# Turning the feed-forward tokens in 32x32 blocks on VectorE, with sixteen DMAs a block, in a macaron transformer layer

## The chip, the cores and the metric

The kernel runs on one core of one Trainium2 chip. The metric is the device time of one execution, in microseconds (us). The five engines of a core (TensorE, VectorE, ScalarE, GpSimd and SyncE; in the profile PE, DVE, ACT, POOL and SP) each run their own instructions in order and wait for each other by semaphores. PEld is TensorE's weight load, and a name with a q at its end (SPq) is an engine's sequencer, which issues DMAs.

## What is computed

A macaron layer in float32 over 16 x 256 tokens of 256 features: half a feed-forward part, attention, another half feed-forward part with the same weights.

```python
x = x + 0.5 * ffn(layernorm(x), w1, b1, w2, b2)
x = x + attention(layernorm(x), Wq, Wk, Wv, Wo)      # 16 heads of 16, causal, rotary
x = x + 0.5 * ffn(layernorm(x), w1, b1, w2, b2)

def ffn(x, w1, b1, w2, b2):        # w1: 1024 x 256, w2: 256 x 1024, both rounded to -1, 0, 1
    h = gelu(x @ ternary(w1).T + b1)
    return h @ ternary(w2).T + b2
```

## The kernel before, in words

The 4096 tokens stay in SBUF through the whole kernel, as 8 blocks (`NBLK`) of 512 tokens (`xs`, line 79): 128 tokens on the partitions, 4 tiles (`BT`) side by side, 256 features in the free dimension. Both feed-forward parts come from one function, `ffn(ln, after)` (line 273), called with ln = 0 and ln = 2. The attention lies between them and is not touched by the change.

A feed-forward part is a sequence of steps `step(u)` (line 373) with u = 8 i + f: block i, and f one of 8 chunks of 128 hidden features. In each step

- `up(i, f)` (line 315) multiplies chunk f of w1 with the block: four matmuls of 128x512 into a PSUM tile m (two such tiles take turns). ScalarE makes the GELU of m twice, as `h_high` (the type float32r, in which TensorE is fast and which keeps fewer bits) and as `h_whole` (float32). VectorE, or GpSimd for f = 1, 3 and 5, subtracts them, which gives `h_rest`, the bits that `h_high` lost.
- `down(i, f - 2)` (line 329) multiplies what was made two steps ago (`LATE` = 2) with w2: eight matmuls of 128x256, tokens as the stationary operand, four token tiles times high and rest. After f = 7 VectorE adds the sum to `xs`, and in the second part two DMAs on SP store the tokens.

The four matmuls of `up` need the tokens of the block the other way round, features on the partitions. The block after the current one is made ready in three places of the steps:

- at f = 3, `prepare(i + 1)` (line 282): four VectorE instructions normalize the four token tiles into `xn`;
- at f = 5 and f = 6, `turn_in(i + 1, k)` (line 291) for the two halves k of the features: TensorE turns four 128x128 squares of `xn` into a PSUM tile `tp`, ScalarE copies `tp` as `high` (`xnT_0`, float32r), VectorE subtracts, which gives `rest` (`xnT_1`);
- `up(i + 1, 0)`, at f = 0 of the next block, is their first reader.

For block 0 of both parts and block 1 of the second part this is called from other places (`begin`, lines 359 to 371, and lines 752 to 771). The steps f = 3, 5 and 6 of blocks 1 to 6 make blocks 2 to 7, in both parts.

All calls go through a wrapper that keeps them in the written order on their engine (`InOrder`, line 159). So an instruction that waits holds back all that stands behind it on its engine. It is also why nearly all instructions have line 167 in the profile, and why they are told apart by their tiles. DMAs are issued by SP, and the framework gives them eight completion semaphores in turn, so that a DMA waits for the one that was issued eight before it.

`flat1` and `flat2` (line 81) are two 128x2048 tiles that first hold the weights w1 and w2 in float32. Later the attention uses `flat1` and the first half of `flat2` for its rotary step (lines 423 to 427); the second half of `flat2` is free once w2 has been rounded, in step 3 of the first part.

Of the kernel before, what the change touches and what calls it, by code (L numbers as in the profile page):

```python
# [8 lines left out]
FP = mybir.dt.float32  # L9
FR = mybir.dt.float32r  # L10
AF = mybir.ActivationFunctionType
# [4 lines left out]
P = 128  # L16
D = 256
KC = D // P
FF = 1024
# [10 lines left out]
def kernel(  # L30
# [17 lines left out]
    BT = 4  # L48
    TB = BT * P
    NBLK = NT // TB  # L50
# [24 lines left out]
    b1_sb = const.tile([P, NFC], FP, name="b1_sb")  # L75
# [5 lines left out]
    flat1, flat2 = (state.tile([P, 2 * FF], FP, name=f"w_{n}") for n in range(2))  # L81
# [19 lines left out]
    for k in range(KC):  # L101
        rows = slice(k * P, (k + 1) * P)
        nc.sync.dma_start(out=wv[:, k, :], in_=wqkvT[rows, 2 * D :])
        for at in range(0, 2 * D, 4 * HD):
            n, j, e = at // D, at // P % 2, at // (4 * HD) % 2
            nc.sync.dma_start(
                out=wqk[:, k, n, j, :, e, :],
                in_=wqkvT[rows, at : at + 4 * HD].rearrange("p (r d) -> p r d", d=HD),
# [20 lines left out]
        out=mask_k,  # L129
        in_=mask_k,  # L130
# [28 lines left out]
    class InOrder:  # L159
# [11 lines left out]
    tensor, vector, scalar, gpsimd, sync = (  # L171
        InOrder(engine) for engine in (nc.tensor, nc.vector, nc.scalar, nc.gpsimd, nc.sync)
    )
# [4 lines left out]
    def stats(ln, n):  # L178
        st = small.tile([P, 6], FP, name="st")
        vector.bn_stats(st, tokens(n))  # L180
        vector.bn_aggr(mv[ln][:, n, :], st)

    def finish_stats(ln, first, n):

        var = small.tile([P, BT], FP, name="var")
        gpsimd.tensor_scalar(
            var[:, 0:n], mv[ln][:, first : first + n, 1], LN_EPS, 1.0, ALU.add, ALU.mult
        )
        gpsimd.tensor_tensor(
            rstd[ln][:, first : first + n], var[:, 0:n], power[:, 0:n], ALU.pow  # L190
        )

    def normalize(ln, n, to, engine=None):
        (engine or vector).tensor_scalar(
            to,
            tokens(n),
            mv[ln][:, n, 0:1],
            rstd[ln][:, n : n + 1],
            ALU.subtract,
            ALU.mult,  # L200
        )
# [30 lines left out]
    def signs(n, of):  # L232

        w, to = of((w1, w2)[n]), of((w1q, w2q)[n])
        vector.tensor_scalar(to, w, half[n][:, 1:2], None, ALU.is_lt)
        vector.scalar_tensor_tensor(
            to, w, half[n][:, 0:1], to.bitcast(FP), ALU.is_gt, ALU.subtract
        )
# [31 lines left out]

    LATE = 2

    def ffn(ln, after):
        xn, xnT, hT, ys = {}, {}, {}, {}

        def measure(i):
            if ln == 0:
                for t in range(BT):
                    stats(0, i * BT + t)
                finish_stats(0, i * BT, BT)  # L280

        def prepare(i, engine=None):
            xn[i] = fp.tile([P, BT, D], FP, name="xn", bufs=1)
            for t in range(BT):
                normalize(ln, i * BT + t, xn[i][:, t, :], engine)
            xnT[i] = [fp.tile([P, KC, TB], FR, name=f"xnT_{n}") for n in range(2)]

        def add_bias(i):
            gpsimd.tensor_add(xs[i], xs[i], b2_sb.unsqueeze(1).to_broadcast([P, BT, D]))

        def turn_in(i, k):
            tp = ps_mm.tile([P, TB], FP, name="mm")
            for t in range(BT):
                tensor.transpose(
                    tp[:, t * P : (t + 1) * P], xn[i][:, t, k * P : (k + 1) * P], ident
                )
            high, rest = (xnT[i][n][:, k, :] for n in range(2))
            scalar.copy(high, tp)
            return lambda: vector.tensor_sub(rest, tp, high.bitcast(FP))

        first = {}

        def up_first(i, f, to=None):
            h = first[i, f] = ps_m.tile([P, TB], FP, name="m") if to is None else to
            for n in range(2):
                for k in range(KC):
                    tensor.matmul(
                        h,
                        w1q[:, k, f * P : (f + 1) * P],
                        xnT[i][n][:, k, :],  # L310
                        start=(n == 0 and k == 0),
                        stop=(n == 1 and k == KC - 1),
                    )

        def up(i, f):
            if (i, f) not in first:
                up_first(i, f)
            h = first.pop((i, f))
            high = fp.tile([P, TB], FR, name="h_high", bufs=LATE + 3)
            rest = fp.tile([P, TB], FR, name="h_rest", bufs=LATE + 3)  # L320
            whole = fp.tile([P, TB], FP, name="h_whole", bufs=3)
            scalar.activation(high, h, AF.Gelu, bias=b1_sb[:, f : f + 1])
            scalar.activation(whole, h, AF.Gelu, bias=b1_sb[:, f : f + 1])

            engine = gpsimd if f in (1, 3, 5) and not (ln == 0 and i == NBLK - 1) else vector
            engine.tensor_sub(rest, whole, high.bitcast(FP))
            hT[i, f] = (high, rest)

        def down(i, f):
            if f == 0 and ln == 2 and i == NBLK - 1:  # L330

                ys[i] = [ps_mm.tile([P, 2, D], FP, name="mm") for t in range(0, BT, 2)]
            elif f == 0:
                y = ps_w.tile([P, BT, D], FP, name="w")
                ys[i] = [y[:, t : t + 2, :] for t in range(0, BT, 2)]
            parts = hT.pop((i, f))
            order = [(t, n) for t in range(BT) for n in range(2)]
            if ln == 2 and (i, f) == (NBLK - 1, NFC - 1):

                order = [(t, n) for n in range(2) for t in range(BT)]  # L340
            for t, n in order:

                tensor.matmul(
                    ys[i][t // 2][:, t % 2, :],
                    parts[n][:, t * P : (t + 1) * P],
                    w2q[:, f, :],
                    start=(f == 0 and n == 0 and t % 2 == 0),
                    stop=(f == NFC - 1 and n == 1 and t % 2 == 1),
                )
            if f == NFC - 1:  # L350
                for t in range(0, BT, 2):
                    xt = xs[i][:, t : t + 2, :]
                    vector.scalar_tensor_tensor(
                        xt, ys[i][t // 2], 0.5, xt, ALU.mult, ALU.add
                    )
                for t in range(0, BT, 2):
                    after(i, t)

        def begin():
            measure(0)  # L360
            if ln == 0:
                sizes(0)
            prepare(0)
            if ln == 0:
                threshold(0)
                signs(0, lambda w: w[:, :, 0 : FF // 2])
            for k in range(KC):
                turn_in(0, k)()
            if ln == 0:
                signs(0, lambda w: w[:, :, FF // 2 :])  # L370
                sizes(1)

        def step(u):
            i, f = divmod(u, NFC)
            if i < NBLK:
                up(i, f)
                if ln == 0 and u == 0:
                    threshold(1)
                if ln == 0 and u in (0, 3):
                    part = slice(0, NFC // 2) if u == 0 else slice(NFC // 2, NFC)  # L380
                    signs(1, lambda w: w[:, part, :])
                if ln == 0 and u == 4:
                    gpsimd.tensor_scalar(b2_sb, b2_sb, 0.5, 0.0, ALU.mult, ALU.add)
                if u == 1:
                    measure(1)
                if ln == 0 and f >= 4 and i + 2 < NBLK:
                    stats(0, (i + 2) * BT + f - 4)
                    if f == NFC - 1:
                        finish_stats(0, (i + 2) * BT, BT)
                if i + 1 < NBLK and (ln, i) != (2, 0):  # L390
                    if f == 3:
                        prepare(i + 1)
                    if f in (5, 6):
                        turn_in(i + 1, f - 5)()
                if f == (1 if i == NBLK - 1 else 6):
                    add_bias(i)
            if u >= LATE:
                down(*divmod(u - LATE, NFC))
            if ln == 0 and u == 2 * NFC + 2:
                make_tables()  # L400
            if ln == 0 and u < (NBLK - 1) * NFC and later:
                later.pop(0)()

        return begin, step, prepare, turn_in, up_first

    FFN_STEPS = NBLK * NFC + LATE
# [12 lines left out]
    xn_a, xnT, qT, kT, o, oT, y_a = {}, {}, {}, {}, {}, {}, {}  # L419
# [326 lines left out]
    rest = []  # L746
    for p in range(8):
# [7 lines left out]
        rest = made  # L755
        if p == 0:
            prepare(0, gpsimd)
    a, z = NB - 2, NB - 1
# [88 lines left out]
```

## Time and profile before

| | us |
|---|---|
| median of three runs | 623.36 (623.34 to 624.16) |
| span of the profiled execution, from the first to the last instruction | 621.8 |
| PE busy | 600.7 (97%) |
| DVE busy | 462.1 (74%) |
| ACT busy | 415.3 (67%) |
| POOL busy | 306.4 (49%) |
| first part, from the first GELU of block 0 to the last GELU of block 7 | 14.5 to 157 |
| second part | 487.3 to 615.7 |
| from the first GELU of a block to that of the next, blocks 3 and 4 of the first part and 2 to 6 of the second | 15.8, 15.8 and 16.1 |

The page lists for each engine how long it was busy. Below it stands the chain of work that ended last, followed back from the last instruction through whatever released each step: engines with a large share there set the time, and time taken from the others gains nothing by itself. The timeline view lists the instructions by start time; in brackets behind an instruction is how long its engine had been idle before it and what ended that.

### The profile page before, as it was taken

What the parts mean: (1) busy time and instruction counts of PE and PEld (TensorE: products, weight loads), DVE (VectorE), ACT (ScalarE), POOL (GpSimd) and SP (SyncE); (2) the same over time, 40 slices, a digit from 0 to 9 for tenths busy, and PEclk for the clock granted to TensorE, in tenths of its full rate; (3) what the DMA queues carried; (4) which work ended last, traced back from release to release, by engine and by line L of the source; (5) the groups of instructions that cost most, each with busy time, mean ns of one, the idle gap of its engine ahead of it and who ended that gap; (6) DMA issues with size and microseconds to landing.
All of it is one profiled execution on the core that took longest, in us unless ns stands there. A gap on an engine that the chain in (4) does not pass through costs nothing.

```text
span 621.8 us, 14721 instructions
## 1 busy us (share of the span) xinstructions
PE 600.7 (97%) x5580; PEld 487.5 (78%) x5580; DVE 462.1 (74%) x1650; ACT 415.3 (67%) x716; POOL 306.4 (49%) x277
## 2 busy tenths in 40 slices
PE   4999999999999999999999999999999999999997
PEld 3798999887667777777777777777766788888886
DVE  6877777785788888888888888888885375555553
ACT  4666766674576667776777677767765666676674
POOL 3655555782464455545564456553442163334443
PEclk9999999999999999999999999999999999999999
DMA  9800000000001000110010001100100011011001
GB/s 286 178 21 1 2 1 18 17 1 18 20 35 38 18 22 35 37 36 21 19 37 36 20 20 36 37 19 21 36 4 2 1 35 35 34 35 35 26 21 56
DMA packets 25478, 21.30 MB, mean 34 GB/s; under 512 B 10944, under 2 KB 21056, under 8 KB 25408
## 3 DMA queue, kind: packets, MB, share of 16 engines
q1 hardware_dynamic: 24848, 19.44, 9.9%
q8 instruction: 44, 0.72, 0.5%
q10 hardware_dynamic: 560, 0.92, 0.4%
q14 instruction: 26, 0.21, 0.1%
HBM read 7.51 MB, written 4.19 MB: 19 GB/s over the span
## 4 chain that ended last, share of the span: by engine, by line
PE 87%; DVE 7%; ACT 2%; issue 2%; POOL 1%; DMA 1%; DVEq 0%; ACTq 0%; POOLq 0%
PE mm L167 37%; PE w L167 28%; PE m L167 21%; DVE h_rest L167 2%; DVE st L167 1%; DVE xn L167 1%; ACT h_high L167 1%; ACT h_whole L167 1%; DVE w2q L167 1%; DMA x<-in_x_dram 1%; DVE mv L167 1%; DVE masked L167 0%; DVE x L167 0%; POOL h_rest L167 0%; POOL rstd L167 0%
## 5 line engine op out<-in xcount | busy, mean ns | idle before, releaser
L167 DVE CUSTOM_DVE_ANT_0 masked<-m,mask_q 128x128 f32<-128x128 f32 x480 | 142.7, 353 | 41.0 <-PE m L167 39.7
L167 PE MATMUL m<-xnT,w1q 128*128 128x512 f32 x504 | 142.5, 404 | 0.9 <-DVE w1q L167 0.9
L167 ACT ACTIVATE h_high<-m,b_sb 128x512 fp32r<-128x512 f32 x126 | 86.7, 688 | 79.2 <-PE m L167 79.2
L167 DVE TENSOR_TENSOR h_rest<-h_whole,h_high 128x512 fp32r<-128x512 f32 x83 | 76.1, 918 | 71.0 <-ACT h_whole L167 70.6
L167 ACT ACTIVATE pT<-w 128x768 f32<-128x768 f32 x128 | 104.1, 814 | 31.6 <-DVE w L167 24.6
L167 PE MATMUL w<-qT,kT 32*128 32x256 f32 (+1 forms) x1024 | 121.7, 349 | 0.8 <-ACT pT L167 0.5
L167 POOL TENSOR_TENSOR h_rest<-h_whole,h_high 128x512 fp32r<-128x512 f32 x45 | 60.3, 1340 | 125.7 <-ACT h_whole L167 125.5
L167 PE MATMUL w<-w2q,h_high 128*128 128x256 f32 x480 | 120.9, 286 | 1.1 <-DVE w2q L167 1.1
L167 PE MATMUL w<-w2q,h_rest 128*128 128x256 f32 x480 | 118.0, 280 | 1.3 <-POOL h_rest L167 1.2
L167 PEld LDWEIGHTS w<-qT,kT 32*128 32x128 f32 x1024 | 90.7, 184 | 32.4 <-issue 26.4
L167 PE MATMUL m<-kT,qT 32*128 32x128 f32 x960 | 114.9, 349 | 0.7 <-ACT kT L167 0.7
L167 PEld LDWEIGHTS m<-xnT,w1q 128*128 128x128 f32 x504 | 86.7, 190 | 16.4 <-DVE xnT L167 2.9
L167 PEld LDWEIGHTS w<-w2q,h_rest 128*128 128x128 f32 x480 | 90.6, 189 | 6.4 <-POOL h_rest L167 1.8
L167 PEld LDWEIGHTS w<-w2q,h_high 128*128 128x128 f32 x480 | 90.4, 188 | 5.8 <-DVE w2q L167 1.6
L167 DVE TENSOR_TENSOR w<-w,mask_k 128x512 f32<-128x512 f32 x128 | 88.9, 695 | 7.1 <-PE w L167 7.1
L167 ACT ACTIVATE h_whole<-m,b_sb 128x512 f32<-128x512 f32 x126 | 85.8, 681 | 0.0
L167 PEld LDWEIGHTS m<-kT,qT 32*128 32x128 f32 x960 | 65.9, 185 | 2.9 <-ACT kT L167 1.6
L167 POOL TENSOR_TENSOR w<-w,cosT 128x512 f32<-128x512 f32 x32 | 41.2, 1289 | 51.9 <-ACT w L167 32.0
L167 PE MATMUL mm<-xnT_a,wqk 128*128 128x256 f32 x256 | 62.2, 386 | 0.0
L167 POOL TENSOR_TENSOR w<-w,sinT 128x512 f32<-128x512 f32 x32 | 40.9, 1278 | 25.7 <-DMA w<-w 25.6
L167 PEld LDWEIGHTS mm<-xnT_a,wqk 128*128 128x128 f32 x256 | 46.2, 190 | 7.6 <-issue 0.7
L167 PE MATMUL mm<-pT,vals 128*32 128x256 f32 (+1 forms) x1024 | 48.2, 329 | 0.3 <-ACT oT L167 0.3
(90 smaller groups left out, 888.0 us busy)
## 6 DMA issues: line engine op xcount, KB each, us to landing
w<-w SPq DMA_DIRECT2D x64, 128.0 KB
out_dram<-x SPq DMA_DIRECT2D x15, 256.0 KB
x<-in_x_dram SPq DMA_DIRECT2D x7, 512.0 KB
w<-in_w2T_dram SPq DMA_DIRECT2D x1, 1024.0 KB
qT<-mT SPq DMA_DIRECT2D x64, 4.0 KB
w<-in_w1T_dram SPq DMA_DIRECT2D x1, 512.0 KB
w<-in_w1T_dram ACTq DMA_DIRECT2D x1, 512.0 KB
wqk<-in_wqkvT_dram SPq DMA_DIRECT2D x16, 32.0 KB
```

The costliest lines, as they stand in the source:

```text
L167: return tc.keep_in_program_order(getattr(self.engine, name)(*args, **kwargs))
```

## The change

For blocks 2 to 7 of both parts (`by_blocks`) TensorE no longer turns the tokens. `prepare` ends with one VectorE instruction that transposes every 32x32 square of `xn` by itself, into the second half of `flat2` (`turned`). Sixteen DMAs on SP then move the squares to where they belong, straight into `xnT_1`; each moves 32 partitions x 2 x 512 bytes, 32 KB. `turn_in` has left a ScalarE copy from `xnT_1` to `high`, and a VectorE subtraction in place on `xnT_1`. The squares arrive in an order in which the tokens of a block are permuted, and the two GELUs put them back by writing through a four-dimensional pattern with runs of 32 elements.

```diff
+    turned = flat2[:, FF:].rearrange("p (j n t) -> p j n t", j=8, n=BT)
+
     def ffn(ln, after):
         xn, xnT, hT, ys = {}, {}, {}, {}
+        by_blocks = range(2, NBLK)
...
             xnT[i] = [fp.tile([P, KC, TB], FR, name=f"xnT_{n}") for n in range(2)]
+            if i in by_blocks:
+                vector.transpose(
+                    turned.rearrange("p j n t -> p (j n t)"),
+                    xn[i].rearrange("p n (j t) -> p j n t", t=32),
+                )
+                for a in range(4):
+                    for j in range(4):
+                        sync.dma_start(
+                            out=xnT[i][1][32 * j : 32 * j + 32, :, a * P : a * P + P].bitcast(FP),
+                            in_=turned[32 * a : 32 * a + 32, j::4, :, :].rearrange(
+                                "p k n t -> p k (n t)"
+                            ),
+                        )
...
         def turn_in(i, k):
+            if i in by_blocks:
+                high, rest = (xnT[i][n][:, k, :] for n in range(2))
+                scalar.copy(high, rest.bitcast(FP))
+                return lambda: vector.tensor_sub(rest, rest.bitcast(FP), high.bitcast(FP))
             tp = ps_mm.tile([P, TB], FP, name="mm")
...
-            scalar.activation(high, h, AF.Gelu, bias=b1_sb[:, f : f + 1])
-            scalar.activation(whole, h, AF.Gelu, bias=b1_sb[:, f : f + 1])
+            for to in (high, whole):
+                if i in by_blocks:
+                    to = to.rearrange("p (n a t) -> p a n t", n=BT, a=4)
+                    of = h.rearrange("p (a n t) -> p a n t", n=BT, a=4)
+                else:
+                    of = h
+                scalar.activation(to, of, AF.Gelu, bias=b1_sb[:, f : f + 1])
```

## The prediction

> **What bounds the kernel now.** I read the page first: busy times, the clock, the chain that ended last.
>
> ```profile
> span 621.8 us, 14721 instructions
> ...
> PE 600.7 (97%) x5580; PEld 487.5 (78%) x5580; DVE 462.1 (74%) x1650; ACT 415.3 (67%) x716; POOL 306.4 (49%) x277
> ...
> PEclk9999999999999999999999999999999999999999
> ...
> PE 87%; DVE 7%; ACT 2%; issue 2%; POOL 1%; DMA 1%; DVEq 0%; ACTq 0%; POOLq 0%
> ```
>
> TensorE is never idle for long and is 87% of the chain. Next, block 3 of the second part: the chain there (start, length), then the timeline of the same stretch (start, time of the group, engine).
>
> ```profile
> 545.17 0.93 PE m L167 x4
> 546.10 0.44 PE mm L167 x4
> 546.54 0.95 PE w L167 x8
> ```
>
> ```profile
> 542.45 1.38 DVE L167 TENSOR_SCALAR xn<-x,mv,rstd 128x256 f32<-128x256 f32 x4
> ...
> 545.94 0.60 PE L167 MATMUL mm<-ident,xn 128*128 128x128 f32 x4
> ...
> 547.30 0.59 ACT L167 CAST xnT<-mm 128x512 fp32r<-128x512 f32 x1
> ...
> 551.49 1.37 PE L167 MATMUL m<-xnT,w1q 128*128 128x512 f32 x4
> ...
> 552.90 0.69 ACT L167 ACTIVATE h_high<-m,b_sb 128x512 fp32r<-128x512 f32 x1 [0.87 <-PE m L167]
> ```
>
> The turning squares (mm) are on the chain: 0.44 us for four. A step without them takes 0.93 + 0.93 = 1.87 us. But look at the dates: the tokens are normalized at 543.83, and the next block's `up` has read them and ended by 552.90. The new path must fit into those 9.1 us. `prepare` stands at f = 3, so only some four steps lie between.
>
> **What is removed.** In 12 blocks (2 to 7, twice) two groups of four squares: 24 x 0.44 = 10.5 us, all on the chain. If everything new were hidden, the time would be 623.4 - 10.5 = 612.9.
>
> **What is added, along its path.** Nothing in the trace turns squares on VectorE or moves 32 KB inside SBUF in 512-byte runs; the nearest DMAs are these, from the SP timeline (first two) and the GpSimd timeline.
>
> ```profile
> 24.99 5.14 SPq L106 DMA_DIRECT2D wqk<-in_wqkvT_dram  x8
> ...
> 170.17 1.15 SPq L167 DMA_DIRECT2D w<-w  x2
> ```
>
> ```profile
> 172.87 1.27 POOL L167 TENSOR_TENSOR w<-w,sinT 128x512 f32<-128x512 f32 x1 [1.41 <-DMA w<-w]
> ```
>
> - *Transpose, 128x1024 float32:* the rows with 1024 elements on VectorE are 0.75 us (tensor_scalar, w1q) and 1.28 (scalar_tensor_tensor, w1q). I take 1.1; ends 0.75 and 2.6 (two passes of the slower row).
> - *Issue:* SP issues one DMA after the other. Of the eight wqk DMAs each also waits on one of the eight completion semaphores in turn, as the new ones will; the quiet ones start 0.55 apart. The pairs inside SBUF take 1.15 for two, the 64 qT ones 0.50 in the median, the output stores 0.37. I take 0.53; ends 0.43 and 0.60. The sixteenth starts 15 x 0.53 = 7.95 us after the first.
> - *Landing:* the second DMA of the pair at 170.17 starts at 170.72, and GpSimd, which waits for it, starts at 172.87: 2.15 for 128 KB. For 32 KB I take 2.0, ends 1.6 and 2.2. All sixteen are needed, as each brings a part of both halves k.
> - *Behind the landing:* ScalarE is in order, so its copy at f = 5 holds back the GELUs of f = 6, those the copy of the second half. Copy 0.59 (the CAST row), two GELUs 1.26 (from 550.76 to 552.02), copy 0.59, VectorE's subtraction 0.69, the last matmul of `up(i + 1, 0)` 0.4: 3.53. A copy from SBUF instead of PSUM, eight semaphores to wait on and the GELUs' output pattern are costed at nothing; the nearest row for SBUF input on ScalarE (qT, 128x256 in 0.50, against 0.37 for the same size from PSUM) makes it up to 0.13 for each copy, and I allow 0.1 for each GELU.
>
> From the end of normalizing to the end of `up(i + 1, 0)`: 1.1 + 0.05 (SP woken) + 7.95 + 2.0 + 3.53 = 14.6 us. Before it is the time from the fourth `xn` to the next block's first h_high. In block 3 of the second part: 543.83 + 14.6 = 558.5 against 552.90, 5.6 late. The same working at each f = 3 gives 7.3, 5.7, 7.3, 7.3, 2.2, 8.2 in blocks 1 to 6 of the first part (block 5 has attention matmuls there for cover; in block 6 normalizing takes until 127.43) and 6.8, then five times 5.6, in the second. Sum: 38.1 + 34.6 = 72.7 us. The removed 10.5 is already in it, as the dates of before hold it.
>
> It does not come back later: the next normalizing stands behind h_rest(2) of the next block on VectorE, so the path closes into a ring once a block. In the gap TensorE has `up(6)`, `up(7)` and `down(5)` left, then waits. Queues: on SP the two stores of a block (540.40) are issued before the sixteen, and the rotary pairs of the first part stand between series with 8 us of room. VectorE's own backlog (some 13 us a block) runs beside the ring.
>
> **The clock.** TensorE will now idle 5 to 7 us a block. What that does is seen at both ends of the trace (PE timeline; then stretches, PEclk third from the end).
>
> ```profile
> 11.86 2.04 PE L167 MATMUL m<-xnT,w1q 128*128 128x512 f32 x4 [0.86 <-DVE w1q L167]
> ...
> 21.16 1.09 PE L167 MATMUL m<-xnT,w1q 128*128 128x512 f32 x4
> ```
>
> ```profile
> 617.20:619.80 2.60, 0.00 (x0) 0.00 (x0) 1.17 (x2) 0.00 (x0) 0.00 (x0) 1.00 0.43 145
> 619.90:621.70 1.80, 0.00 (x0) 0.00 (x0) 0.00 (x0) 0.00 (x0) 0.00 (x0) 0.50 0.19 64
> ```
>
> Less than 2.8 us after the last matmul the granted clock is 0.50. At the start matmuls begin 0.43 us apart until 15.7 us and 0.23 after, that is, 3.9 us from the first dense ones, 7.5 from TensorE's first instruction. So after each gap some 4 us pass at half speed and lose 2.0; ends 0 and 3.7 (the two steps between `up(i + 1, 0)` and the next h_rest(2) at half speed, after which the loss is hidden). 12 x 2.0 = 24 us.
>
> Sum against the profiled execution: 621.8 + 72.7 + 24 = 718.5. The median stands 1.6 above the span (what lies around it), which gives **720 us**.
>
> Two rules of the Trainium skill bear on this. In "DMA: Bandwidth & Descriptors", section "Issuing engines are not separate DMA queues", the sequencer's time to start a DMA is called usually small beside the DMA; the rows say otherwise here (0.53 x 16 against one landing of 2). Taken at its word, with issue free, the path would be 8 us shorter, no block late, and the time 613. The same page's rules for kernel authors speak against the change: transfers under 64 KB are mostly overhead. "TensorE: Matmul & The Clock Gate", Part 1, has the clock fall after one idle window of about 3.4 us and rise after one such busy window; by it the loss would be 1.7 to 3.4 a gap, 20 to 41 in all, where the rows gave 24.
>
> **Rivals.**
> - *Hidden after all, faster: 612.9.* It decides by the issue pace: with the mean lateness of 6.1 us a block, it breaks even at 0.53 - 6.1 / 15 = 0.12 us a DMA and no clock loss. No row is under 0.37. 5%.
> - *Late, but the clock holds* (idle cut up by the GELUs and first matmuls, or issue at 0.43 and a shorter landing): 621.8 + 72.7 + 1.6 = 696, with the fast issue down to 680. For it: `up(6)` and `up(7)` still fall into the gap. Against it: what is left of the gap is twice the 2.8 us. 20%.
> - *The ring of semaphores sets the pace:* each DMA waits for the eighth before it, and where landings grow longer SP slows down. The eight wqk DMAs from 16.76 on took 7.64 us, 0.95 apart, beside the big loads. That would add 15 x 0.42 = 6.3 a block, 76 in all: 796. Against it: SBUF is quiet then, and eight issues last 4.2 us, twice a landing. 12%.
> - *The change does not do it:* the instruction order of the changed kernel shows the 24 groups gone from PE, twelve transposes on DVE and 192 DMAs on SP. No more than 1% for a time within 0.2%, about what a measurement of this kernel can tell from no change.
>
> **Numbers.** Forecast 62%, and with the second rival 82%. The range takes in both, the unknown ends above (issue 0.60: +12; transpose 2.6: +18; clock: +20, not all at once) and stops short of the ring: 680 to 765. Faster 5%, same 1%, slower 94%.
>
> **What would show it.** SP's sixteen issues lasting 8 us or more (if 2 us, I am wrong at the root); ScalarE's copy waiting for DMA, 5 us or more; PE idle before `up(i + 1, 0)` twelve times; matmuls 0.43 apart behind each gap, PEclk at 5 or between; blocks of 15.8 and 16.1 us grown to some 24; attention as long as before.

## The result, and the profile after

| | us |
|---|---|
| before, median | 623.35 (623.32 to 624.16) |
| after, median of four runs | 744.73 (742.47 to 745.12) |
| ratio after / before | 1.193 [1.192, 1.195] |
| profiled execution of after | 742.47, span 740.7 |

The kernel is 19% slower; the forecast was 720 us, in a range of 680 to 765. The page of after, in the lines that were shown of before and with the row of TensorE's slices:

```profile
span 740.7 us, 14986 instructions
...
PE 617.8 (83%) x5484; PEld 498.3 (67%) x5484; DVE 462.4 (62%) x1662; ACT 415.0 (56%) x716; POOL 301.9 (41%) x277
...
PE   5949648668599999999999999999999477558657
...
PEclk9989779789699999999999999999999797889789
...
PE 67%; SPq 15%; DVE 6%; ACT 5%; DMA 4%; issue 3%; POOL 1%; ACTq 0%; DVEq 0%; POOLq 0%
```

The same row of TensorE's slices before:

```profile
PE   4999999999999999999999999999999999999997
```

Read the slices (the busy share of each fortieth of the span, in tenths) from left to right: TensorE and its clock have holes at both ends, in the two feed-forward parts, and are untouched in the middle, in the attention. The row of the chain names what came in: SP's sequencer, which had no share before, has 15% of the span, and DMA went from 1% to 4%. TensorE has fewer matmuls (96 squares less) and is still busy for longer, as part of it ran at a lower clock.

One block, the chain of after from the end of the transpose on (start, length, what):

```profile
627.35 0.95 PE w L167 x8
628.29 0.58 SPq L167
628.87 0.05 issue
628.92 0.59 SPq L167
...
637.23 0.59 SPq L167
637.82 0.04 issue
637.87 1.89 DMA xnT<-w
639.75 0.02 issue
639.78 0.62 ACT xnT L167
640.39 0.59 ACT h_high L167
640.98 0.59 ACT h_whole L167
641.57 0.04 issue
641.61 2.16 PE m L167 x4
```

From 628.29 to 637.82 the chain is SP and nothing else: sixteen times 0.59 us and a gap of 0.045. Then one landing, the copy, the two GELUs that stand behind it, and TensorE. The timeline of the same stretch shows how long the others waited (in brackets):

```profile
626.97 1.25 DVE L167 STREAM_TRANSPOSE w<-xn 128x1024 f32<-128x1024 f32 x1
...
628.28 10.18 SPq L167 DMA_DIRECT2D xnT<-w  x16
...
639.78 0.62 ACT L167 CAST xnT<-xnT 128x512 fp32r<-128x512 f32 x1 [9.26 <-DMA xnT<-w]
...
641.61 2.16 PE L167 MATMUL m<-xnT,w1q 128*128 128x512 f32 x4 [7.73 <-ACT h_whole L167]
```

And over the whole kernel, in the view of waits (total, times, longest):

```profile
ACT xnT L167 <- DMA xnT<-w: 123.6, 12, 12.9
...
PE m L167 <- ACT h_whole L167: 102.1, 12, 9.9
```

Twelve waits of ScalarE, twelve of TensorE behind them: one for each block from the third on, in both parts. TensorE's wait is put down to `h_whole`, a GELU, but the GELU itself was late only because the copy before it on ScalarE had waited for the DMA. The name in a wait is the last link and not the cause.

### The profile page after: what moved, and what is told of

The parts are those of the page before. It is cut to its first block, busy times and chain, and to the rows that moved or that the text cites. A ratio compares the mean times of both kernels' runs of the same rounds, so it can differ in the third digit from the quotient of the medians.

```text
span 740.7 us, 14986 instructions
## 1 busy us (share of the span) xinstructions
PE 617.8 (83%) x5484; PEld 498.3 (67%) x5484; DVE 462.4 (62%) x1662; ACT 415.0 (56%) x716; POOL 301.9 (41%) x277
## 4 chain that ended last, share of the span: by engine, by line
PE 67%; SPq 15%; DVE 6%; ACT 5%; DMA 4%; issue 3%; POOL 1%; ACTq 0%; DVEq 0%; POOLq 0%
PE mm L167 30%; PE w L167 21%; PE m L167 16%; SPq L167 15%; DMA xnT<-w 3%; ACT h_high L167 1%; ACT h_whole L167 1%; DVE h_rest L167 1%; ACT xnT L167 1%; DVE st L167 1%; DMA w<-in_w1T_dram 1%; DVE xn L167 1%; DVE xnT L167 1%; DVE w2q L167 1%; DVE masked L167 0%
## 5 line engine op out<-in xcount | busy, mean ns | idle before, releaser
L167 PE MATMUL m<-xnT,w1q 128*128 128x512 f32 x504 | 160.5, 443 | 103.4 <-ACT h_whole L167 102.1
L167 PEld LDWEIGHTS m<-xnT,w1q 128*128 128x128 f32 x504 | 96.4, 208 | 126.4 <-ACT h_whole L167 104.5
L167 PE MATMUL w<-w2q,h_rest 128*128 128x256 f32 x480 | 125.6, 292 | 2.3 <-DVE h_rest L167 1.4
L167 PE MATMUL w<-w2q,h_high 128*128 128x256 f32 x480 | 126.9, 295 | 0.2 <-DVE w2q L167 0.2
L167 PEld LDWEIGHTS w<-w2q,h_rest 128*128 128x128 f32 x480 | 97.3, 203 | 9.0 <-DVE h_rest L167 2.0
L167 PEld LDWEIGHTS w<-w2q,h_high 128*128 128x128 f32 x480 | 97.6, 203 | 5.9 <-DVE w2q L167 0.8
L167 DVE TENSOR_TENSOR h_rest<-h_whole,h_high 128x512 fp32r<-128x512 f32 x83 | 63.7, 767 | 59.8 <-ACT h_whole L167 59.6
L167 DVE TENSOR_TENSOR xnT<-xnT,xnT 128x512 fp32r<-128x512 f32 x24 | 16.4, 683 | 128.0 <-ACT xnT L167 128.0
L167 ACT CAST xnT<-xnT 128x512 fp32r<-128x512 f32 x24 | 14.8, 617 | 123.6 <-DMA xnT<-w 123.6
L167 POOL TENSOR_SCALAR var<-mv 128x4 f32<-128x4 f32 (+1 forms) x32 | 7.2, 225 | 123.8 <-DVE mv L167 123.3
```

Source lines behind the costliest of these rows:

```text
L167: return tc.keep_in_program_order(getattr(self.engine, name)(*args, **kwargs))
```

## The experiments

The theory on trial: sixteen issues, one behind the other on SP, are on the path from normalizing to the next block, and what the path lacks TensorE waits, once a block. The rivals: the added work costs as such (VectorE, SBUF traffic, the GELUs' pattern); the landing or the semaphores set the pace, not the issue; most of it is the clock. In the first, fifth and sixth of these kernels there is work whose result nothing reads. All figures beside "after" go by its median or, for spans and stretches, by its profiled execution.

**All the added work, and nobody waits for it.** TensorE turns the squares as before; the transposes and the 192 DMAs are made as well, into a tile that nothing reads. The GELUs write in plain order, and `h_high` and `h_rest` have four buffers instead of five, which makes room.

```diff
+                shadow = fp.tile([P, KC, TB], FR, name="shadow", bufs=1)
...
-                            out=xnT[i][1][32 * j : 32 * j + 32, :, a * P : a * P + P].bitcast(FP),
+                            out=shadow[32 * j : 32 * j + 32, :, a * P : a * P + P].bitcast(FP),
...
-            if i in by_blocks:
-                high, rest = (xnT[i][n][:, k, :] for n in range(2))
...
-                if i in by_blocks:
+                if False:
```

> Everything that the change adds is still done (12 VectorE transposes, 192 DMAs), but the sixteen DMAs land in a scratch tile that nobody reads, and TensorE turns the tokens as before; the GELUs write without the permuting pattern, and h_high and h_rest have four buffers instead of five to make room. Theory (the time is lost in waiting for the sixteen DMAs, which SP starts one after the other): the wait is gone, so 623 to 628 us, near the kernel before, with no ScalarE wait for these DMAs. Rival (the added work itself, on VectorE, the DMA engines or SBUF, slows the others): 680 us or more.

Measured: 624.45 us (623.93 to 625.74), ratio 1.0015 [1.0005, 1.0025]. SP's timeline of one block:

```profile
545.38 10.59 SPq L167 DMA_DIRECT2D shadow<-w  x16
556.77 0.98 SPq L762 DMA_DIRECT2D out_dram<-x  x2
```

The sixteen DMAs take as long as in after, with TensorE busy for 97% of the span. So neither the transposes nor the traffic cost anything to speak of (1.2 us by the medians); the loss lies in waiting for them and in what the waits bring. The GELUs' pattern is not in this run. The pace of the issue is SP's own, as no one holds it up here and it is no faster.

**Twice as many DMAs of half the size.** One of 16 KB for each half k.

```diff
-                        sync.dma_start(
+                        for k in range(KC):
+                            sync.dma_start(
...
```

> Each of the sixteen DMAs is split into its two halves: 32 DMAs a block of 16 KB, the same bytes in the same 512-byte runs, same result. Theory (the number of DMAs times SP's 0.64 us for each is the price): 16 x 0.64 = 10.2 us more in each of 12 blocks, 122 in all, so 860 to 880 us, with SP's series lasting some 21 us. Rival (bytes or packets in flight are the price): within 10 us of the changed kernel's 745.

Measured in one run: 852.18 us, span 850.4; a little under the 860 to 880 expected, and far from the rival's 745.

```profile
667.36 21.02 SPq L167 DMA_DIRECT2D xnT<-w  x32
...
ACT xnT L167 <- DMA xnT<-w: 234.1, 12, 23.0
```

A DMA of 16 KB took 0.589 us of SP in the median, one of 32 KB 0.595: the price goes by the DMA, not by its bytes. SP's time doubled with the number. In the mean of a series, one starts 0.631 to 0.666 after the other; in after it is 0.638 to 0.701. With 32 in a series, 24 of them use a semaphore again that an earlier one of the series had, and the pace is the same: the ring of eight semaphores does not set it. The path grew by 9.3 us a block, a little less than sixteen issues, because the copy of the first half no longer waits for the last DMA: it starts 1.2 us after the last DMA's start, where it was 2.0.

**Started earlier.** From block 1 on `prepare` stands at f = 0 instead of f = 3.

```diff
-                    if f == 3:
+                    if f == (0 if i else 3):
                         prepare(i + 1)
```

> One edit to the changed kernel: prepare stands at f = 0 instead of f = 3 (for block 1 of the first part as before), so the path starts about three steps earlier. Theory (a ring of normalizing, transpose, sixteen issues, landing, copies, first up; what lies between first up and the next normalizing shrinks from some 8.7 us to 2 or 3): some 6 us less in each of 12 blocks, 655 to 685 us, and TensorE's gap down to 2 to 4 us. Rival (the added load slows the others): no change, 745.

Measured in one run: 683.7 us, span 681.9. The timeline of a block of the second part:

```profile
581.95 1.25 DVE L167 STREAM_TRANSPOSE w<-xn 128x1024 f32<-128x1024 f32 x1
...
583.25 10.18 SPq L167 DMA_DIRECT2D xnT<-w  x16
...
594.86 0.62 ACT L167 CAST xnT<-xnT 128x512 fp32r<-128x512 f32 x1 [4.58 <-DMA xnT<-w]
...
596.70 2.12 PE L167 MATMUL m<-xnT,w1q 128*128 128x512 f32 x4 [3.05 <-ACT h_whole L167]
```

The series is as long as ever (10.18), the path from the last `xn` to the first GELU of the next block still 16.7 to 17.7 us in the second part (up to 19.0 in the first). But in five of the six blocks there it begins 3.28 us after a block's first GELU, where it was 7.5 to 8.7, and what begins earlier is late by less: TensorE waits 3.05 instead of 7.73 here. These blocks take some 20 to 21 us, which is the path and the 3.28 before it. It closes into a ring, as the prediction had it.

**On two sequencers.** ScalarE issues every second DMA.

```diff
-                        sync.dma_start(
+                        (sync, scalar)[j % 2].dma_start(
```

> The changed kernel with every second of the sixteen DMAs issued by ScalarE instead of SP. Theory (the price is each sequencer's own 0.64 us a DMA): SP's series shrinks from 10 to 5 us, ScalarE loses some 5 us a block at f = 3 but lies idle in the gap anyway; the path gets 4 to 5 us shorter and TensorE's gap too, so 680 to 700 us. Rival (the two sequencers share what makes a DMA slow to start, so that 16 still take 10 us): 735 to 760.

Measured in one run: 708.25 us, span 706.4.

```profile
605.52 5.13 ACTq L167 DMA_DIRECT2D xnT<-w  x8
605.56 5.38 SPq L167 DMA_DIRECT2D xnT<-w  x8
...
610.70 0.69 ACT L167 ACTIVATE h_high<-m,b_sb 128x512 fp32r<-128x512 f32 x1 [6.64 <-DMA xnT<-w]
...
612.01 1.42 PE L167 MATMUL m<-xnT,w1q 128*128 128x512 f32 x3 [4.60 <-ACT h_whole L167]
```

Both sequencers issue at the same time, in this block 0.65 us (ScalarE) and 0.68 (SP) from one start to the next. That the same bytes in the same sixteen DMAs go out in half the time excludes a limit in the DMA engines behind them. The time is above the 680 to 700 expected, and the third and fourth lines show why: while ScalarE issues it makes no GELU, so those of the chunks under way come late, and TensorE has its gap there instead.

**The clock, first try.** 28 matmuls that nothing reads stand at the end of f = 7, to keep TensorE busy through the gap.

```diff
+            if f == NFC - 1 and i + 1 in by_blocks:
+                idle = ps_mm.tile([P, TB], FP, name="mm")
+                for n in range(28):
+                    tensor.matmul(
+                        idle, w1q[:, 0, 0:P], xnT[i][0][:, 0, :], start=True, stop=True
+                    )
```

> 28 further matmuls of 128x512 that nobody reads stand at the end of f = 7 in each of the 12 blocks, where TensorE waits 8 to 10 us; at full clock they last 6.5 us. Theory (after each gap TensorE runs at half clock, which costs 1 to 1.5 us a block): the granted clock stays near 1, and the time falls by 10 to 20 us, to 725 to 735. Rival (the clock is hidden in the ring): 743 to 746. If the matmuls reach past the end of the gap: more than 745.

Measured: 741.83 us (741.46 to 746.72), ratio to before 1.190 [1.188, 1.192], which is 2.9 us under after by the medians, where 10 to 20 were expected. By parts of the profiled execution (746.72, the slowest of the five) it is not the same: the blocks of the second part lost 6.3 us less in all, those of the first 10.7 more. There two things spoil it: single issues took up to 2.04 us, and block 5, whose gap is only 6.3 us, has its `up` held up by the extra matmuls themselves, some 5 us. As an answer for all twelve blocks it is inconclusive, so the next one asks it of the second part alone.

**The clock, second try.** 31 extra matmuls, in the six gaps of the second part alone.

```diff
+            if ln == 2 and f == NFC - 1 and i + 1 in by_blocks:
+                idle = ps_mm.tile([P, TB], FP, name="mm")
+                for n in range(31):
```

> The changed kernel with 31 further matmuls that nobody reads in each gap of the second part alone (six gaps), the first part as in the changed kernel. Theory (the slow clock behind a gap costs 1 to 1.5 us a block; in the earlier run with such matmuls in both parts this was masked in the first part): granted clock 1.0 through the second part, its blocks at 23.6 us instead of 25 to 26, and 734 to 739 us in all. Rival (no price of the clock): 744 to 746.

Measured: 734.72 us (733.72 to 735.6), ratio to before 1.178 [1.175, 1.180]: 10.0 us under after, 1.67 a gap (by the spans of the two profiled executions, 740.7 and 733.2, 1.25 a gap). The same 150 us of both kernels, first after, then this one (busy time of PE, PEld, DVE, ACT and POOL with counts, then granted clock, DMA share and GB/s):

```profile
575.00:725.00 150.00, 100.20 (x555) 87.74 (x555) 49.33 (x79) 64.13 (x105) 36.52 (x24) 0.83 0.14 40
```

```profile
575.00:725.00 150.00, 144.41 (x801) 120.61 (x801) 54.30 (x85) 69.91 (x114) 42.17 (x27) 1.00 0.15 43
```

With the gaps filled the clock stays at 1.00, and VectorE, whose work has not changed, gets 54.3 us done in this stretch instead of 49.3. So the clock is a loss of its own beside the wait, of 1.25 to 1.67 us a gap.

**A block ahead.** Now the cover: `prepare` is called for block i + 2 instead of i + 1, with a third buffer for `xnT_1`. Block 2 of the first part is turned by TensorE, so that eleven blocks are left; `h_high` and `h_rest` have four buffers.

```diff
-        by_blocks = range(2, NBLK)
+        by_blocks = range(3 if ln == 0 else 2, NBLK)
...
+                if f == 4 - ln // 2 and i + 2 in by_blocks:
+                    prepare(i + 2)
```

> The new path made a block ahead: prepare(i + 2) in step f = 4 of block i in the first part (its statistics moved to f = 0 to 3) and f = 3 in the second, so that 9 to 10 steps (17 to 19 us) lie between normalizing and the ScalarE copy at f = 5 of block i + 1; a third buffer of xnT_1, four buffers of h_high and h_rest. Block 2 of the first part stays with TensorE, so 11 blocks go the new way. Theory (only the wait costs): path 1.3 + 1.25 + 9.9 + 2.0 = 14.5 us fits, no gaps, clock at 1, and what the change removes shows: 11 x 2 x 0.44 = 9.7 us less than the kernel before, 612 to 617 us. Rival (the issue or the DMAs collide with something else on SP, rotary pairs and stores): between 623 and 660.

Measured: 627.50 us (626.59 to 630.08), ratio 1.008 [1.006, 1.010]. All but 4 of the 121 us are back, with the work of the change still done in eleven blocks of twelve: the loss was the waits and the clock's fall behind them. ScalarE's copies no longer wait for a DMA at all, so the rival, a collision on SP, did not come. But TensorE, which has 22 groups of squares less to do, is not faster for it. The timeline of a block of the second part says why:

```profile
549.82 2.85 POOL L167 TENSOR_TENSOR x<-x,b_sb 128x1024 f32<-128x1024 f32 x1
...
550.34 2.88 DVE L167 TENSOR_TENSOR h_rest<-h_whole,h_high 128x512 fp32r<-128x512 f32 x1
...
553.15 0.68 DVE L167 TENSOR_TENSOR xnT<-xnT,xnT 128x512 fp32r<-128x512 f32 x1
...
553.88 0.50 PE L167 MATMUL m<-xnT,w1q 128*128 128x512 f32 x1 [1.39 <-DVE xnT L167]
```

A subtraction of this shape takes 0.69 us. This one takes 2.88 and ends at 553.22, 0.55 after GpSimd's bias addition (552.67); the `xnT` that the next block needs stands behind it, and TensorE waits 1.39 us.

**The bias addition moved out of the way.** First with the last kernel (`add_bias` at f = 1 instead of 6, block 2 of the first part turned a step later), then alone in the kernel before.

```diff
-                if f == (1 if i == NBLK - 1 else 6):
+                if f == (6 if (ln, i) == (0, 0) else 1):
```

> The kernel made a block ahead (the run before this one of that kind, 627.5 us), with GpSimd's add_bias at f = 1 instead of f = 6 (block 0 of the first part as it was), and block 2 of the first part turned at f = 3 and 4. Theory (in the second part VectorE's subtractions at f = 5 and 6 now read SBUF alone and are held for 2.9 us while GpSimd adds the bias, which left TensorE a gap of 1.4 us a block): the gap goes and the second part runs at 8 x 1.87 = 15.0 us a block instead of 16.6, the whole at 614 to 620 us, faster than the kernel before. Rival (the gap comes from the copy waiting for DMA or from VectorE's own load): 626 to 629.

> The kernel before with only add_bias moved from f = 6 to f = 1 (block 0 of the first part as it was): what this edit is worth without the change. Theory: TensorE's wait for xnT there is 0.28 us a block in the second part, so 620.5 to 623.5 us, 0 to 2.5 less. Rival (the edit itself is the gain of the version made a block ahead): 615 to 619.

Measured: 627.6 us (627.49 to 628.12), ratio 1.007 [1.006, 1.009], and 634.02 (632.72 to 634.18), ratio 1.017 [1.015, 1.018]. In the first of the two, blocks 2 to 6 of the second part take 15.6 us (16.1 before) and TensorE's waits for `xnT` there, 8.3 us in all a block ahead, are gone, as hoped, but the second and third interval of the first part, the ones from block 1's and block 2's first GELU on, take 18.7 and 21.1 (15.8 and 16.9 before). In the kernel before, the move costs 10.7 us by itself: 4.1 of it in the same third interval (20.95), 3.2 in the last two of the first part and 2.9 in the first of the second. So the loss in the third interval of the other kernel is the price of the bias addition's new place. The 2.9 us in its second interval are not: the move alone costs 0.4 there, and the cause was not looked for. So 627.6 lies where the rival had it, but not for the rival's reason, and 634.02 is outside of both expectations. GpSimd's addition meets a VectorE subtraction at its new place as well:

```profile
547.73 2.41 POOL L167 TENSOR_TENSOR x<-x,b_sb 128x1024 f32<-128x1024 f32 x1
...
548.25 2.44 DVE L167 TENSOR_TENSOR h_rest<-h_whole,h_high 128x512 fp32r<-128x512 f32 x1 [0.94 <-ACT h_whole L167]
```

Here too VectorE ends 0.55 us after GpSimd (550.69 and 550.14). Only what stands behind it has changed.

**The best of these.** A block ahead, with the bias at f = 1 in blocks 1 to 7 of the second part alone; in block 1 of the first part block 2 is normalized at f = 0 and turned at f = 3 and 4, and block 3 prepared at f = 5.

```diff
-                if f == (1 if i == NBLK - 1 else 6):
+                if f == (1 if i == NBLK - 1 or ln == 2 and i > 0 else 6):
```

> The kernel made a block ahead once more: add_bias stays at f = 6 in the first part and stands at f = 1 in blocks 1 to 7 of the second alone; block 2 of the first part is normalized at f = 0, turned at f = 3 and 4, and block 3 made ready at f = 5 of block 1. Theory (path hidden, and the best place of GpSimd's bias in each part by the two versions before: first part 15.2 us a block with f = 6, second 15.6 with f = 1): 618 to 622 us, a little faster than the kernel before (623.3). Rival (what is saved on TensorE is given back to VectorE and GpSimd holding each other wherever the bias stands): 623 to 628.

Measured: 623.19 us (621.77 to 624.9), ratio 0.999 [0.998, 1.000], no difference that can be told, and above the 618 to 622 expected. In the profiled execution (624.9, the slowest of the twelve) the blocks are shorter where nothing waits (15.2 us instead of 15.8 in two of the first part, 15.6 instead of 16.1 in the second), and the first part gives it back in two places. The interval from block 2 of the first part on takes 17.85 instead of 16.87, with TensorE waiting 1.30 us for `h_rest` at 48.7. Block 7 has its last GELU 24.9 us after its first, before 21.9; TensorE waits 1.04 us there at 140.4, for an `h_rest` on VectorE, and a little later its clock falls (same columns as above):

```profile
142.50:145.90 3.40, 3.40 (x13) 2.90 (x12) 1.42 (x9) 1.17 (x2) 0.00 (x0) 0.50 0.00 0
```

No version here is faster than the kernel before by a difference that can be told. The clock seems to have a part in that: the five executions with a mean granted clock of 0.998 or more took 621.8 to 622.6 us, the seven at 0.993 to 0.997 took 623.1 to 624.9. Whether the two places could be mended as well was not tried, and how much of block 7's 3 us is VectorE's order and how much the clock stays open.

## Why the prediction was right, and where it was short

Sign and mechanism were right: twelve waits, one a block, behind SP's sixteen issues, which neither the tokens' bytes nor the added work explain (first two experiments). The blocks of after take 24.9 to 28.5 us from first GELU to first GELU, where some 24 were forecast, and the attention as long as before, 330.9 us from the last `h_high` before it to the first behind it. The size was 22 us short by spans (718.5 forecast, 740.7 in the profiled execution), 25 by the medians (720 and 744.73). By spans, 118.9 us were lost and 96.7 forecast; by terms:

| term, over 12 blocks | forecast | measured |
|---|---|---|
| transpose (1.1 each; 1.25) | | +1.8 |
| SP woken (0.05; 0.09) | | +0.5 |
| fifteen starts (0.53 apart; 0.657) | | +22.9 |
| landing (2.0; 1.9 to 2.2) | | +0.5 |
| behind the landing (3.53; 4.28) | | +9.0 |
| lateness from all of these | 72.7 | 107.5 |
| what is left of the 118.9, set against the clock | 24 | 11.4 |

The measured lateness is the time from the end of normalizing to the first GELU of the next block, summed over twelve blocks, 210.4 us, less the 102.9 of the same stretches before; the five rows above are how much each part of the path differs from its forecast, and come to 34.7 of the 34.8 us between 72.7 and 107.5. The last row is a remainder and not a measurement of the clock. That the sum missed by 22 and not by 35 is luck: the path's terms were 34.8 too small, and the clock's 12.6 too large.

- **Removed, 10.5 us:** right as a sum of instructions. It needs all the cover there is to be seen: even with the waits gone, one block ahead, the kernel was 4 us slower than before.
- **Issue, 0.53, mostly from the wqk DMAs:** this is the term that was mis-sized. SP took 0.595 for each and 0.045 between two, and the sum ran at 0.64 to 0.70. The range of 0.43 to 0.60 that I gave did not even hold it. The other rows at hand were nearer: the pairs inside SBUF take 0.57 for each, and the second DMA of a pair, which starts behind another as all but one of the sixteen do, 0.588 in the median. It is multiplied by 180, so each hundredth is 1.8 us.
- **Landing, 2.0, and transpose, 1.1:** both close (1.9 to 2.2 and 1.25), from rows of other shapes.
- **Behind the landing, 3.53:** the copies were costed right (0.62 from SBUF, 0.59 from PSUM), the GELUs' pattern rightly at nothing (h_high 689 ns in the mean, 688 before). What was missed is the end: `up(i + 1, 0)` itself runs at the half clock that the gap leaves behind (its four matmuls take 2.16 in the timeline above, and 1.83 with the gaps filled), from its last matmul to the GELU it is 0.9 us and not 0.4, and VectorE's second subtraction ends 0.8 us after its copy in the second part and 1.3 in most of the first, where 0.69 was forecast.
- **The gap and the clock:** TensorE's gaps were 6.3 to 9.9 us and not 5 to 7, as the path is longer. In the block shown the clock fell at 639, 5 us after the last matmul, and rose at 645.7, after 4.1 us of matmuls at half speed; that is the 4 us of the forecast. Over the twelve gaps it is 3.1 to 5.8 us. The price measured by filling the gaps is lower than the forecast's 2.0, 1.25 to 1.67 a gap, 0.33 of it in the end of the path. Where the rest lies can be read off: from a block's first GELU to the next normalizing's end it takes 7.5 to 8.7 us in five blocks of the second part of after, and 7.0 in the kernel before and with the gaps filled. That it is not more because waits of other engines hide it is my reading and was not tried. For the first part no run shows the price. In "TensorE: Matmul & The Clock Gate", Part 1, the Trainium skill has one idle window and one busy one of about 3.4 us; my estimate by it was 1.7 to 3.4 a gap, and the runs lie at or under the lower end. The stretches at 0.50 behind the twelve gaps last 6.8 or 10.2 us, once 13.7, which agrees with whole windows of that length.
- **The rivals.** *The ring of semaphores* did not come: the pace was the same with 16 and 32 DMAs, and in the chain the gap in front of each issue is 0.04 to 0.05 throughout the block shown. *The clock holds* did not come: granted 0.83 in the stretch of the second part above. *Hidden after all* was wrong as the change stands, and the row that decides it is the issue pace, 0.64 and not 0.12. Given the cover by hand, a block ahead, it still did not give 612.9: in the second part VectorE, held up by GpSimd's bias addition, took the place of the wait (1.39 us a block), and what held the first part back was not cleared up in full.

Of the Trainium skill's "DMA: Bandwidth & Descriptors" the runs speak against the rule on issue ("Issuing engines are not separate DMA queues") and for the one on small transfers ("Rules for kernel authors"). Issue was not small beside the DMA: 0.595 us of the sequencer, sixteen times, for one landing of 2. And the small transfers were indeed mostly overhead: a DMA of 16 KB took SP as long as one of 32 KB, and 32 KB took 1.9 to 2.2 us to land, where the prediction read 2.15 for 128 KB.

## What to carry to other kernels

Price a series of DMAs by their number times what the sequencer takes for one of the nearest kind in the trace, and lay that beside the time from the data's being ready to its first reader; if it is longer, the engine waits in every round, as here with 32 KB and with 16 KB a DMA. Work taken off the engine that bounds is a gain only if what replaces it is started early enough, and then look at who waits for whom between the engines that took it over: here that ate most of what was left. A gap in TensorE of 6 to 10 us cost its length here and then the clock's fall, also for the matmuls that end the gap.

## What the runs showed of the hardware

- **VectorE is held by GpSimd when both work from SBUF.** In four places a VectorE subtraction with both inputs in SBUF started while GpSimd ran, and ended 0.55 us after it: 2.88 us instead of 0.69 (a block ahead), 2.44 (bias at f = 1), 1.95 for `h_rest` in the kernel before at 549.75, 1.44 for an `xnT` at 548.98 in the kernel a block ahead. It is the rule there: in the kernel before, all 14 subtractions of `h_rest` that started during a bias addition ended so. It does not go for every instruction of GpSimd: beside `rstd` (128x4, 1.02 us from 32.84) the one at 33.09 took its usual 0.69. The subtraction with one operand in PSUM (`xnT<-mm`, 547.91 in the kernel before) took its usual 0.69 beside a GpSimd subtraction from 547.48 to 548.78. The change turns the second kind into the first. The Trainium skill, "SBUF — State Buffer", section "SBUF: two separate sides", calls this an exclusive lock on a shared pair of ports, which whoever starts first keeps for the whole instruction. The rows beside bias and `h_rest` agree with it, the one beside `rstd` does not, for a reason that no run shows.
- **The clock can fall without a long gap too.** In the last kernel it was at 0.50 for 3.4 us from 142.5 on (the line above) and again from 470.2 on, in the attention. In the 3.4 us before these TensorE was busy for 2.16 and 2.86 us by the profile, with longest gaps of 1.04 and 0.54. What share of idle time it takes was not tried.
- **Some issues are long.** Of 192 in after, three took far more than 0.595 us, up to 1.45; of the 192 in the first clock experiment six, up to 2.04. Beside each of these nine a 16 KB packet of the instruction queue was under way; beside the one at 604.26 in after, from 604.0 to 605.3. That the one holds up the other is argued from the times alone.
